# A state space stage with y kept transposed, D x added on TensorE, and its instructions emitted in the order of a list scheduler

## The chip, the cores and the metric

The kernel runs on one core of a Trainium2 chip. The metric is device time in microseconds (us) of one execution; the profile gives one profiled execution. Engines are named as in the profile: PE is TensorE (matmuls; PEld are its weight loads), DVE is VectorE, ACT is ScalarE, POOL is GpSimd, SP is SyncE, which here only issues DMAs. All data is fp32. In the trace every matmul of fp32 operands appears as two records, a transpose as one.

## The reference, cut to what matters

The input has 2 images of 256 channels and 48 x 48 positions. Layer 0 adds a local attention and depthwise convolutions. Layer 1 treats each image as 2304 tokens of 256 channels. It adds a state space model to the normalised tokens and then a mixture of 8 experts of which each token uses two. What the change touches is the state space model:

```python
xn = rmsnorm(x)                                   # x: (2, 2304, 256)
zxbcdt = einsum('bld,ed->ble', xn, W_in)
z, xBC, dt = zxbcdt[..., :512], zxbcdt[..., 512:1152], zxbcdt[..., -8:]
conv = sum(pad(xBC)[:, k:k + L, :] * conv_w[:, k] for k in range(4)) + conv_b
xBC = silu(conv)                                  # 512 of x, 64 of B, 64 of C
dt = softplus(dt + dt_bias)                       # 8 heads of 64 channels
dA = exp(dt * -exp(A_log))
state = state * dA_t + (dt_t * x_t) B_t           # scan over tokens
y_t = state C_t
y = (y + Dp * xs) * silu(z)
y = rmsnorm(y, gnorm_w, 1e-5)
out = x + einsum('ble,de->bld', y, W_out)
```

The experts follow on the normalised result: a gate picks the two experts of each token, and each expert is two matrix products with a gelu between them.

## The kernel before, in words

`run` has three stages that follow one another: `layer0`, `mamba` and `experts`. The change is in `mamba` and in a few lines around it.

`mamba` works on 12 blocks (`NBLK` 6 for each of two images) of 384 tokens, and each block on 3 chunks of 128 tokens, 36 chunks in all. Six front stages work on a block:

- `norms` (L590) transposes 3 x 2 pieces of the residual on PE, copies them out on ACT (L541), takes means and variances on DVE, and writes the new residual (L612) and the normalised tokens (L618) on DVE.
- `project_0` and `project_1` transpose the normalised tokens back, multiply by the weights of x, B and C (five products of 387 columns by `project`, L553), and do the four taps of the convolution: the last on ACT (L662), three on DVE (L666). Then come two silus on ACT (L649, L650). A DMA moves the rows of C to partitions 0 to 63 (L652).
- `gates_0` and `gates_1` compute z, dt and the gate's scores for each chunk, tokens on partitions: 2 x 2 products of 264 columns, a silu from PSUM (L679), and two small DVE operations (L683, L684); then `softplus` for dt.
- `sums` makes the cumulated decays with three small products and two exponentials.

Six stages work on a chunk:

- `token_stage` makes `al` on POOL (L744), transposes B and x on PE (L748, L751), copies them out on ACT (L753, L755), makes `xd` on DVE (L757) and `xw` and y = D x on POOL (L759, L761).
- `decay_stage` multiplies `al` by a triangle (two products of 512 columns, L769), takes the exponential on ACT (L778, `mt`), and multiplies by the masked B C product on DVE (L779).
- `state_stage` makes this chunk's addition to the state (L787) and the old state's part of y (L790), decays and adds the state on DVE (L795, L796) and scales the part of y on DVE (L798); POOL adds it to y (L799).
- `y_stage` is eight heads of 64 columns with `mt` as the weights (L808), an addition on DVE (L809), the product with z on POOL (L810), squares with a sum on ACT (L813), and an inverse root by `rsqrt` (L171 on DVE, L172 on POOL).
- `turn_stage` transposes y in four pieces (L539) and copies it on ACT (L541).
- `out_stage` multiplies by `W_out` and the gate's folded weights (L835, 264 columns), adds to the residual on DVE (L839), adds the gate's scores (L840), takes statistics (L844, L845), and stores the chunk by DMA (L846).

`gate` works on a group of 6 chunks (the last two groups have 3). It takes the two best experts of each token with some thirty small DVE operations, writes the normalised tokens (L871), counts with two small products (L905, L906), numbers the rows (L915, L916), and sends each chunk by two indirect DMAs that POOL issues (L926), 72 in all. `experts` begins with `plan` on those counts and reads the rows back.

What sets the order: in `mamba` a loop of steps calls the stages with written lags (front stages up to five steps ahead, `out_stage` four behind) and draws from the generator `gate` between them. The framework places every instruction on its engine's queue from this order and may move it; the engines then work through their queues in order and wait for semaphores. PSUM has 4 single banks and 2 pairs, shared by all three stages.

Of the kernel before, what the change touches and what calls it, by code (L numbers as in the profile page):

```python
# [30 lines left out]
F32 = mybir.dt.float32  # L31
# [5 lines left out]
P = 128  # L37
# [20 lines left out]
ZH = DI // 2  # L58

ZG = ZH + SH  # L60
XBC = 2 * ZG
# [4 lines left out]
GRP = 6  # L66
# [15 lines left out]
for _name, _k in (  # L82
    ("bq", NH), ("bk", NH), ("bv", NH), ("bp", 1), ("w1", NH * 9), ("w2", NH * 9), ("norm_w", NH),
    ("gnorm_w", DI // P), ("conv_w", NM * 4), ("conv_b", NM),
):
    _VEC[_name] = (_n, _n + _k)
    _n += _k
# [4 lines left out]
for _name, _k in (  # L92
    ("dt_bias", SH), ("A_log", SH), ("Dp", SH), ("bg", E), ("rate1", 1), ("rate2", 1),
):
    _ROW[_name] = (_n, _n + _k)
    _n += _k
# [17 lines left out]
def together(*streams):  # L114

    streams = list(streams)
    while streams:
        for s in list(streams):
            if next(s, StopIteration) is StopIteration:
                streams.remove(s)  # L120
        yield


def interleave(*streams):
    for _ in together(*streams):
        pass


class Kernel:
# [12 lines left out]


    def setup(self):
        nc, ins = self.nc, self.ins
        self.ps = self.pool("ps", 4, space=bass.MemoryType.PSUM)
        self.ps2 = self.pool("ps2", 2, space=bass.MemoryType.PSUM)
# [27 lines left out]
    def layer0(self, ctx):  # L175


        nc, ins, v, r = self.nc, self.ins, self.v, self.r
        wts = self.pool("l0w", 1, ctx)
# [314 lines left out]
    def mamba_weights(self):  # L494
# [4 lines left out]
        wout = wts.tile([P, DI // P, C + E], F32, name="wout")  # L499
# [5 lines left out]
        self.l1 = dict(win=win, wout=wout, na=na, sw=sw)  # L505

    def scale_weights(self):
# [3 lines left out]
        wg = [l1["win"][:, k, ZG + ZH : XBC] for k in range(NH)]  # L511
# [4 lines left out]
        for k in range(NH):  # L516
            for w in (l1["win"][:, k, : ZG + ZH], l1["win"][:, k, XBC:]):
                nc.gpsimd.tensor_scalar(w, w, v["norm_w"][:, k : k + 1], None, ALU.mult)
        turned = self.att.tile([P, NH, P], F32, tag="turned", name="turned", bufs=1)
        for m in range(DI // P):  # L520
# [34 lines left out]
    def mamba(self, ctx):  # L555


        self.m = self.pool("m", 2, ctx)
        self.blocks, self.chunks = {}, {}
        nblk, nchunk = B * NBLK, B * NBLK * NJ  # L560
        front = (self.norms, self.project_0, self.project_1, self.gates_0, self.gates_1, self.sums)
        stages = ((self.out_stage, 4), (self.turn_stage, 3), (self.y_stage, 2), (self.state_stage, 1),
                  (self.decay_stage, 1), (self.token_stage, 0))
        groups = [GRP] * (nchunk // GRP - 1) + [GRP // 2] * 2
        starts = [sum(groups[:n]) for n in range(len(groups))]
        gate = iter(())
        for step in range(-NJ * 2, nchunk + 4):
            for p in reversed(range(len(front))):
                k, r = divmod(step + len(front) - 1 - p, NJ)
                if r == 0 and 0 <= k < nblk:  # L570
                    front[p](k)
                    next(gate, None)
            for stage, lag in stages:
                c = step - lag
                if 0 <= c < nchunk:
                    if stage == self.out_stage and c in starts:
                        self.group = dict(first=c, n=groups[starts.index(c)])
                    stage(c)
                next(gate, None)
            done = step - 3  # L580
            if done in starts[1:] or done == nchunk:
                for _ in gate:
                    pass
                gate = self.gate(self.group)
        for _ in gate:
            pass


    def norms(self, k):

        nc, small = self.nc, self.small
        b, blk = divmod(k, NBLK)
        t = self.m.tile([P, NJ, C], F32, tag="t", name="t", bufs=2)
        st = small.tile([P, NJ, 6], F32, tag="lst", name="lst")
        mv = small.tile([P, NJ, 2], F32, tag="lmv", name="lmv")
        for j in range(NJ):
            cols = slice(blk * TB + j * P, blk * TB + (j + 1) * P)
            self.transposes(t[:, j, :], [self.x[b][:, h, cols] for h in range(NH)])
            nc.vector.bn_stats(st[:, j, :], t[:, j, :])
            nc.vector.bn_aggr(mv[:, j, :], st[:, j, :])  # L600
        mean, var = mv[:, :, 0], mv[:, :, 1]
        rs, ms, rr, rs1, mrs, kap = (
            small.tile([P, NJ], F32, tag=f"n{name}", name=name) for name in ("rs", "ms", "rr", "rs1", "mrs", "kap")
        )
        self.rsqrt(rs, var, 1e-5)
        nc.vector.tensor_mul(ms, rs, rs)
        nc.vector.tensor_mul(ms, ms, var)
        self.rsqrt(rr, ms, F32_EPS)
        nc.vector.tensor_scalar(rs1, rs, 1.0, None, ALU.add)
        nc.vector.tensor_mul(mrs, mean, rs)  # L610
        for j in range(NJ):
            nc.vector.tensor_scalar(  # L612
                self.residual(k * NJ + j), self.halves(t[:, j, :]), rs1[:, j : j + 1], mrs[:, j : j + 1],
                ALU.mult, ALU.subtract,
            )
        nc.vector.tensor_mul(rr, rr, rs)
        for j in range(NJ):
            nc.vector.tensor_scalar(  # L618
                t[:, j, :], t[:, j, :], mean[:, j : j + 1], rr[:, j : j + 1], ALU.subtract, ALU.mult
            )  # L620

        nc.vector.reciprocal(kap, rr)
        nc.vector.tensor_mul(kap, kap, rs1)
        msw = small.tile([P, NJ, E], F32, tag="msw", name="msw")
        nc.vector.tensor_tensor(msw, bcast(mean, 2, [P, NJ, E]), bcast(self.l1["sw"], 1, [P, NJ, E]), ALU.mult)
        self.blocks[k] = dict(t=t, kap=kap, msw=msw)

    def project_0(self, k):
        nc, block = self.nc, self.blocks[k]
        t = block.pop("t")  # L630
        xn = block["xn"] = self.m.tile([P, NH, TB + 3], F32, tag="xn", name="xn")

        if k % NBLK == 0:
            nc.vector.memset(xn[:, :, 0:3], 0.0)
        else:
            nc.vector.tensor_copy(xn[:, :, 0:3], self.blocks[k - 1]["xn"][:, :, TB:])
        for h in range(NH):
            self.transposes(xn[:, h, 3:], [t[:, j, h * P : (h + 1) * P] for j in range(NJ)])
        block["xc"] = self.m.tile([P, NM - 1, TB], F32, tag="xc", name="xc")
        block["bc"] = self.m.tile([P, TB], F32, tag="bc", name="bc", bufs=3)  # L640
        for m in range(2):
            self.convolve(block, m)

    def project_1(self, k):
        nc, block = self.nc, self.blocks[k]
        for m in range(2, NM):
            self.convolve(block, m)
        xc, bc = block["xc"], block["bc"]
        nc.scalar.activation(xc, xc, AF.Silu)  # L649
        nc.scalar.activation(bc, bc, AF.Silu)  # L650
        ct = block["ct"] = self.m.tile([DS, TB], F32, tag="ct", name="ct", bufs=3)
        nc.sync.dma_start(ct, bc[DS:P, :])  # L652

    def convolve(self, block, m):

        nc = self.nc
        xn, win = block["xn"], self.l1["win"]
        ps = self.bank()
        self.project(ps[:, : TB + 3], lambda k: win[:, k, XBC + m * P : XBC + (m + 1) * P], lambda k: xn[:, k, :])
        wc = self.v["conv_w"][:, 4 * m : 4 * m + 4]  # L660
        out = block["xc"][:, m, :] if m < NM - 1 else block["bc"]
        nc.scalar.activation(  # L662
            out, ps[:, 3 : TB + 3], AF.Identity, bias=self.v["conv_b"][:, m : m + 1], scale=wc[:, 3:4]
        )
        for i in range(3):
            nc.vector.scalar_tensor_tensor(out, ps[:, i : i + TB], wc[:, i : i + 1], out, ALU.mult, ALU.add)  # L666

    def gates(self, block, j):

        nc = self.nc  # L670
        xn, win = block["xn"], self.l1["win"]
        cols = slice(3 + j * P, 3 + (j + 1) * P)
        ps = self.banks()
        for h in range(2):
            self.project(
                ps[:, h, :ZG], lambda k: xn[:, k, cols], lambda k: win[:, k, h * ZG : (h + 1) * ZG]
            )
        z = block["z", j] = self.m.tile([P, DI], F32, tag="z", name="z", bufs=7)
        nc.scalar.activation(z.rearrange("p (h q) -> p h q", h=2), ps[:, :, :ZH], AF.Silu)  # L679
        if j == 0:  # L680
            block["dt"] = self.small.tile([P, NJ, SH], F32, tag="dt", name="dt")
            block["gp"] = self.small.tile([P, NJ, E], F32, tag="gp", name="gp")
# [577 lines left out]
```

## Time and profile before

| what | value |
|---|---|
| three timed runs: median (lowest to highest) | 1681.74 us (1681.54 to 1685.04) |
| profiled execution: time, span of its instructions | 1685.3 us, 1683.5 us |
| mean granted PE clock | 0.924 |
| busy over the span: PE, PEld, DVE, ACT, POOL | 1443.4, 1090.4, 926.1, 706.6, 580.6 us |
| first copy of `norms` to the first product of the experts (L541 to L1082) | 385.7 to 1073.1 us, so 687.4 us |
| busy from 385 to 1080 us: PE, PEld, DVE, ACT, POOL | 563.6, 371.4, 504.6, 308.4, 394.6 us |
| granted PE clock from 385 to 1080 us | 0.88 |

The span lies inside the time of the execution; 1.8 us lie around it. Busy time of PE counts records that overlap once; it depends on the granted clock, at which a product of the same shape takes up to twice as long. The experts take the span from 1073 us on and PE is busy there nearly without a gap.

### The profile page before, as it was taken

The page shows a single profiled execution, that of the slowest core. Times are in us where ns is not written, and L with a number is a line of the kernel's source. Part 1 is how long each engine was busy: PE and PEld are TensorE (multiplying, and loading weights), DVE is VectorE, ACT ScalarE, POOL GpSimd, SP SyncE. Part 2 cuts the span into 40 slices and gives each one's busy share as a digit, 9 for nine tenths or more (in the row PEclk, how much of TensorE's full clock was granted, in tenths as well). Part 3 has the DMA queues.
Part 4 walks back from the last instruction along what each step waited for, and adds up shares of the span by engine and source line. Part 5 has one row for each costly group of instructions (what it writes and reads, how often), then busy time and mean ns, then how long its engine had stood idle before and what let it go on. Part 6 is the DMA issues. An engine that isn't in the chain of part 4 may idle for free.

```text
span 1683.5 us, 20769 instructions
## 1 busy us (share of the span) xinstructions
PE 1443.4 (86%) x7188; PEld 1090.4 (65%) x7188; DVE 926.1 (55%) x2359; ACT 706.6 (42%) x1554; POOL 580.6 (34%) x596
## 2 busy tenths in 40 slices
PE   3788897877899889698897984499999999999994
PEld 1556565655556556465654653488888888888884
DVE  6688798985787868679687774211111111112113
ACT  0658584875655446355353520123223222322320
POOL 4111100201466565655656666221222122122220
PEclk9889998997999899798898976799999999999997
DMA  5312122211000010100101002577667666666747
GB/s 198 112 56 68 51 86 70 75 47 56 3 10 12 9 51 10 40 18 9 48 12 38 20 10 71 187 219 240 205 195 233 213 199 213 227 204 201 222 109 231
DMA packets 75689, 180.04 MB, mean 107 GB/s; under 512 B 8172, under 2 KB 66429, under 8 KB 69117
## 3 DMA queue, kind: packets, MB, share of 16 engines
q1 hardware_dynamic: 55660, 152.95, 26.3%
q0 software_dynamic: 14976, 20.26, 6.4%
q10 hardware_dynamic: 4948, 5.51, 1.0%
q8 instruction: 57, 0.93, 0.2%
q14 instruction: 48, 0.39, 0.1%
HBM read 140.40 MB, written 44.41 MB: 110 GB/s over the span
## 4 chain that ended last, share of the span: by engine, by line
PE 58%; DVE 18%; POOL 10%; ACT 7%; DMA 3%; issue 3%; SPq 0%; DVEq 0%; ACTq 0%; POOLq 0%
PE bank L1082 16%; PE po L1096 16%; PE bank L553 4%; DVE x L309 4%; POOL xs L926 3%; PE banks L553 3%; PE bank L808 2%; PE bank L835 2%; PE bank L539 2%; DVE hid L309 2%; PE bank L483 2%; ACT prob L440 2%; PE banks L769 1%; DVE prob L428 1%; PE bank L790 1%
## 5 line engine op out<-in xcount | busy, mean ns | idle before, releaser
L1086 ACT ACTIVATE hid<-bank,wt 128x256 f32<-128x256 f32 (+1 forms) x352 | 159.9, 455 | 405.2 <-PE bank L1082 401.3
L1082 PE MATMUL bank<-ext,wt 128*128 128x256 f32 (+1 forms) x1408 | 286.7, 362 | 2.6 <-DMA wt<-in_We 1.8
L1102 POOL DMA_INDIRECT acc<-ey,ex x80 | 124.9, 1562 | 463.6 <-DVE ey L1100 346.3
L1096 PE MATMUL po<-wt,hid 128*128 128x256 f32 x1280 | 283.7, 379 | 0.0
L1082 PEld LDWEIGHTS bank<-ext,wt 128*128 128x128 f32 x1408 | 250.1, 191 | 34.0 <-DVE ey L1100 2.1
L1096 PEld LDWEIGHTS po<-wt,hid 128*128 128x128 f32 x1280 | 239.8, 190 | 30.8
L541 DVE COPY ext<-bank 128x512 f32<-128x512 f32 (+1 forms) x44 | 28.3, 643 | 233.5 <-PE bank L539 233.5
L440 ACT ACTIVATE prob<-prob,top 128x308 f32<-128x308 f32 x144 | 78.4, 550 | 83.9 <-DVE top L428 83.8
L1099 DVE TENSOR_TENSOR ey<-po,wt 128x256 f32<-128x256 f32 x80 | 34.0, 424 | 143.8 <-PE po L1096 143.7
L309 DVE SCALAR_TENSOR_TENSOR x<-hid,w2r,x 128x1128 f32<-128x1128 f32 (+3 forms) x72 | 99.6, 1383 | 4.1 <-ACT hid L312 2.6
L553 PE MATMUL bank<-xn,win 128*128 128x387 f32 x240 | 95.4, 542 | 3.2 <-ACT xn L541 2.9
L360 POOL COPY kp<-kp 128x10 f32<-128x10 f32 (+1 forms) x60 | 22.5, 375 | 218.4 <-DVE kp L355 218.4
L483 PE MATMUL bank<-pt,val 110*64 110x128 f32 (+1 forms) x864 | 75.5, 297 | 23.0 <-DVE x L488 19.0
L666 DVE SCALAR_TENSOR_TENSOR xc<-bank,vec,xc 128x384 f32<-128x384 f32 x144 | 81.7, 611 | 21.4 <-ACT xc L662 20.9
L553 PE MATMUL banks<-win,xn 128*128 128x264 f32 x288 | 90.4, 449 | 0.0
L483 PEld LDWEIGHTS bank<-pt,val 110*64 110x64 f32 (+1 forms) x864 | 64.4, 147 | 39.2 <-DVE x L488 20.5
L926 POOL DMA_INDIRECT xs<-u,rows x72 | 75.6, 1051 | 35.2 <-issue 19.1
L309 DVE SCALAR_TENSOR_TENSOR hid<-xp,vec,hid 128x1128 f32<-128x1128 f32 (+3 forms) x64 | 87.3, 1374 | 0.3
L810 POOL TENSOR_TENSOR y<-y,z 128x512 f32<-128x512 f32 x36 | 47.0, 1306 | 107.2 <-DVE y L809 34.0
L744 POOL TENSOR_TENSOR al<-cst,a 128x1024 f32<-128x1024 f32 x36 | 68.6, 1913 | 42.1 <-DVE taken L916 14.1
L769 PE MATMUL banks<-al,cst 128*128 128x512 f32 x144 | 78.0, 641 | 5.3 <-ACT mt L778 4.7
L553 PEld LDWEIGHTS bank<-xn,win 128*128 128x128 f32 x240 | 50.6, 215 | 40.7 <-issue 9.5
(247 smaller groups left out, 2606.2 us busy)
## 6 DMA issues: line engine op xcount, KB each, us to landing
wt<-in_We SPq DMA_DIRECT2D x44, 2184.0 KB
ex<-xs SPq DMA_DIRECT2D x36, 265.0 KB
val<-vtab SPq DMA_DIRECT2D x72, 110.0 KB
x<-in_x SPq DMA_DIRECT2D x4, 1152.0 KB
vraster<-vout SPq DMA_DIRECT2D x18, 256.0 KB
acc<-x SPq DMA_DIRECT2D x36, 128.0 KB
vtab<-vraster SPq DMA_DIRECT2D x12, 304.0 KB
val<-vtab SPq DMA_DIRECT2D x36, 88.0 KB
```

The lines of the kernel that those rows point to most:

```text
L309: nc.vector.scalar_tensor_tensor(dst, src, w[:, k : k + 1], dst, ALU.mult, ALU.add)
L440: nc.scalar.activation(prob[:, a, :], prob[:, a, :], AF.Exp, bias=top[:, a : a + 1], scale=-1.0, accum_out=den[:, a : a + 1],)
L483: nc.tensor.matmul(po[j * HD : (j + 1) * HD, :P], lhsT=val[:nk, i, a * HD : (a + 1) * HD], rhs=pt[:nk, j, i, :], start=i == 0, stop=i == l ...
L553: self.nc.tensor.matmul(ps, lhsT=lhs(k), rhs=rhs(k), start=k == 0, stop=k == NH - 1)
L666: nc.vector.scalar_tensor_tensor(out, ps[:, i : i + TB], wc[:, i : i + 1], out, ALU.mult, ALU.add)
L744: nc.gpsimd.tensor_tensor(al, bcast(self.c["le"], 1, [P, SH, P]), bcast(block["a"][:, j, :], 2, [P, SH, P]), ALU.mult)
L769: nc.tensor.matmul(pd[:, k, :], lhsT=self.c["gt"], rhs=al[:, 4 * k : 4 * k + 4, :].rearrange("p s t -> p (s t)"), start=True, stop=True,)
L926: put = nc.gpsimd.indirect_dma_start(self.xs, bass.IndirectOffsetOnAxis(ap=rows[:, i, k : k + 1], axis=0), u2[:, i, :], None)
L1082: nc.tensor.matmul(ps[:, :rows], lhsT=w1[:, k, c * P : (c + 1) * P], rhs=xt[:, k, :], start=k == 0, stop=k == NH - 1,)
L1086: nc.scalar.activation(hid[:, c, :], ps[:, :rows], AF.Gelu, bias=b1[:, c : c + 1])
L1096: nc.tensor.matmul(po, lhsT=hid[:, c, j * P : (j + 1) * P], rhs=w2[:, c, :], start=c == 0, stop=c == NHC - 1)
L1102: put = nc.gpsimd.indirect_dma_start(self.acc, bass.IndirectOffsetOnAxis(ap=token, axis=0), y, None, compute_op=ALU.add)
```

## The change

In words, by the names of the new code:

- **y has its channels on partitions.** `y` is four pieces of 128 channels by 128 tokens. `py` takes `xd` as the weights (64 columns) and `mt` as the moving side (128 columns), two heads of a pair into the two halves of the output's partitions. D x is added in the same PSUM bank by a product with a diagonal matrix (`diag`, made once). z is computed with channels on partitions (four products of 384 columns for a block). `turn_stage`, the POOL operations L761 and L799 and the copy `xt` are gone.
- **The sum of squares** is taken by PE (`ss`: four products of one column with the squares as weights).
- **The state** lies on 128 partitions by 256 columns; its decay is on POOL (`decayed`). The old state's part of y is four products (`ps`). Its decay in time now varies along the free axis; it is made by a small product (`er`), an exponential (`from`), a store of 8 x 384 values to DRAM (`spread`), and two broadcasting loads for a chunk (`rd`, 256 KB).
- **Moves to ACT**: the residual (`sr`), the normalised tokens (`st`) and the gate's normalised tokens (`u2`), which were DVE's L612, L618 and L871.
- **dt and scores** of a block are one group of three 16-column products (`dg`).
- **ACT's tables**: the six silus of a block are a chain that nothing interrupts, and the table with exp and ln is loaded after it.
- **PSUM** pools are made for each stage; in `mamba` 4 single banks, 1 pair and 2 banks for z. **Groups** of the gate are 6, 6, 6, 6, 6, 4, 2.
- **Order**: every operation is added to `Flow` with an engine, a cost in ns, what it needs, and which buffers it takes and frees. `run` plays the engines forward in time and emits each operation when its engine is free, the most urgent first. For PE, DVE and ACT the framework keeps this order (`manual_schedule`); POOL and the DMA queues are not in that list.

The core of the diff:

```diff
-GRP = 6
+GROUPS = (6, 6, 6, 6, 6, 4, 2)
+class Flow:
+    HOP = 120
+    def rank(self):
...
+            tail[k] = o["cost"] + max(same, default=0) + self.HOP
+        return {k: o["due"] - tail[k] for k, o in self.ops.items()}, after
+    def run(self):
...
+            for k in sorted(ready, key=lambda k: rank[k]):
+                o = ops[k]
+                if ready[k] > now or busy.get(o["engine"], 0) > now:
+                    continue
+                kinds = [kind for kind, _ in o["takes"]]
+                if any(free[kind] < kinds.count(kind) for kind in kinds):
+                    continue
...
+                o["make"]()
 def mamba(self, ctx):
+        room = dict(bank=4, banks=1, zbank=2, cvbank=1, t=2, xn=2, xc=2, bc=3, ct=3, z=2, al=2, btt=2, xd=3, xw=2,
+                    mt=2, gm=2, y=4, sq=2, state=3, rd=3, u2=2)
...
+        with self.tc.manual_schedule(
+            engines={mybir.EngineType.PE, mybir.EngineType.DVE, mybir.EngineType.Activation}
+        ):
+            self.flow.run()
+    PACE = 11000
...
+        op("al", "POOL", 1940, al, ("s5", k), takes=[("al", c)])
+        op("pd", "PE", 880, pd, ("al", c), takes=[("banks", ("pd", c))], uses=[("al", c)])
+            def from_state():
+                ps, old = [self.bank_for(("ps", c, g)) for g in range(2)], T["state", c - 1]
+                for m in range(2):
+                    for g in range(2):
+                        rows = slice(g * DS, (g + 1) * DS)
+                        nc.tensor.matmul(
+                            ps[g][:, m * P : (m + 1) * P], lhsT=old[rows, m * P : (m + 1) * P],
+                            rhs=(T["bc", k][rows, cols] if g else T["ct", k][:, cols]), start=True, stop=True,
+                        )
...
+            op("rd", "queue", 2800, rd, ("spread", k), takes=[("rd", c)])
+            op("ps", "PE", 450, from_state, ("state", c - 1), ("ct", k), ("rd", c), takes=[("bank", ("ps", c, 0)), ("bank", ("ps", c, 1))],
+               uses=[("state", c - 1)] + ([("bc", k)] if last else []))
+            op("decayed", "POOL", 750, decayed, ("state", c - 1), ("ex", k), takes=[("state", c)],
+               uses=[("state", c - 1)])
+        def py():
+            ps = self.bank_for(("py", c))
+            for m in range(NZ):
+                part = slice(m * P, (m + 1) * P)
+                for i in range(2):
+                    s = 2 * m + i
+                    nc.tensor.matmul(
+                        ps[i * HD : (i + 1) * HD, part], lhsT=T["xd", c][:, s * HD : (s + 1) * HD],
+                        rhs=T["mt", c][:, s, :], start=True, stop=False,
+                    )
+                nc.tensor.matmul(
+                    ps[:, part], lhsT=self.l1["diag"][:, m, :], rhs=T["xc", k][:, m, cols], start=False, stop=True
+                )
...
+        op("py", "PE", 1800, py, ("mm", c), ("xd", c), None if fresh else ("yi", c), takes=[("bank", ("py", c))],
+           uses=[("mt", c), ("xd", c)] + ([("xc", k)] if last else []))
...
+        op("ss", "PE", 880, ss, ("sq", c), takes=[("bank", ("ss", c))], uses=[("sq", c)])
+        op("out", "PE", 920, out, ("yz", c), ("rs", c), takes=[("bank", ("out", c))], uses=[("y", c)])
+                op(("put", (c, q)), "POOL", 1100, put, ("g10", g), ("g8", g), ("u2", c), ("number", c), uses=[("u2", g)])
```

A chunk's operations are due at 11 us times its number (`PACE`), and a group's gate at the time of its last chunk plus three.

## The prediction

> **What bounds the kernel now.** I first read the busy time over the span, then the busy time in stretches of the state space stage, cut where a group of 6 chunks ends.
>
> ```profile
> PE 1443.4 (86%) x7188; PEld 1090.4 (65%) x7188; DVE 926.1 (55%) x2359; ACT 706.6 (42%) x1554; POOL 580.6 (34%) x596
> ```
>
> ```profile
> core 0: us, PE busy (x) PEld busy (x) DVE busy (x) ACT busy (x) POOL busy (x), PEclk, DMA share, GB/s
> 385.00:561.00 176.00, 155.35 (x650) 100.37 (x649) 133.87 (x355) 99.55 (x169) 83.13 (x69) 0.92 0.06 21
> 561.00:669.00 108.00, 91.51 (x389) 60.48 (x388) 83.97 (x227) 51.50 (x88) 66.20 (x60) 0.92 0.08 25
> 669.00:775.50 106.50, 90.48 (x385) 59.40 (x384) 79.87 (x225) 50.90 (x88) 64.95 (x60) 0.90 0.08 25
> 775.50:883.40 107.90, 92.54 (x388) 60.16 (x387) 82.83 (x227) 51.09 (x88) 66.26 (x59) 0.91 0.08 25
> 883.40:993.00 109.60, 93.64 (x392) 60.30 (x390) 83.80 (x210) 45.76 (x77) 77.00 (x70) 0.91 0.08 25
> 993.00:1073.00 80.00, 33.17 (x126) 24.88 (x125) 37.87 (x171) 6.37 (x15) 37.01 (x39) 0.62 0.18 60
> ```
>
> The columns are the stretch, its length, and busy time by engine, then PE's granted clock. In the four middle stretches PE is the busiest, 85%, but at clock 0.91. Busy time times clock is PE's work at full clock: 84.2, 81.4, 84.2 and 85.2 us, mean 83.8, so 13.96 us for a chunk, while a chunk takes 432 / 24 = 18.0 us. For 36 chunks the work is 503 us, and the stage lasts 687.4 us (385.7 to 1073.1). So 185 us are PE standing or PE slow: about 33 in the first stretch (176 less 155.35 x 0.92), 97 in the middle ones (432 less 335), 55 in the tail. That is all that a better order can win.
>
> Where it stands shows in the timeline. POOL first, then PE, at the end of a group:
>
> ```profile
> 698.63 1.09 POOL L926 DMA_INDIRECT xs<-u,rows  x1 [0.92 <-DVE rows L923]
> 700.02 0.96 POOL L926 DMA_INDIRECT xs<-u,rows  x1 [0.30 <-issue]
> ...
> 709.86 1.27 POOL L810 TENSOR_TENSOR y<-y,z 128x512 f32<-128x512 f32 x1
> ```
>
> ```profile
> 704.60 0.27 PE L748 MATMUL bank<-cst,bc 64*128 64x64 f32 x1
> 712.33 1.11 PE L751 MATMUL bank<-cst,xc 128*128 128x128 f32 x4 [7.46 <-DVE gm L776]
> ```
>
> The gate's 12 indirect DMAs stand in one row on POOL, 1.27 us each. The chunks' own POOL work waits behind them, and PE stands 7.5 us. What follows is slow as well. The same eight heads, before and after a pause of 9 us:
>
> ```profile
> 1009.99 1.90 PE L808 MATMUL bank<-xd,mt 128*128 128x64 f32 x16
> ...
> 1026.17 3.51 PE L808 MATMUL bank<-xd,mt 128*128 128x64 f32 x16
> ```
>
> **The change, PE's work.** I take the distance of starts of consecutive matmul records at full clock. 128x128 transposes: 0.109 us. 264 columns: 0.222. 387 columns: 0.325. 64 columns behind 128-column weights (L808): 0.112, so this is the least that a full weight load costs. Two products in different halves of the weight columns (L483, 128 columns) come 0.057 apart, half of 0.109, so they run side by side. So do two in different halves of the rows: the score products (L422) start 0.006 apart in pairs. A step from whole columns to half columns costs: L464 to L464 is 0.109, L464 to L483 0.202, so 0.093 for a switch. For a chunk:
>
> - transposes of y go: 4 x 0.109 = -0.44;
> - z, dt and scores, for a block: 24 x 0.222 = 5.33 become 16 x 0.322 (L329, 384 columns) + 12 x 0.112 = 6.50; by three, +0.39;
> - `er`: 6 x 0.109 for a block, +0.22;
> - state (L787: 0.48 + 0.52) becomes two pairs of 256 columns (0.215 by L1082) = 0.43, -0.57; the old state's part (L790: 0.53 + 0.43) becomes four pairs of 0.109, -0.52;
> - `py`: 16 x 0.112 = 1.79 become 16 x 0.057 + 8 x 0.109 + 8 switches x 0.093 = 2.52, +0.73;
> - `ss`: eight weight loads of 0.112, +0.90.
>
> Together +0.71 us, by 36 = +26 us: PE's work is 528 us, 14.67 for a chunk. No record shows a burst of four half-column products between switches; between full overlap without switch cost (-27 us) and no overlap (16 x 0.052 x 36 = +30 us) I take the rows as they stand.
>
> **The other engines**, for the stage. DVE (504.6 us) loses L612 13.1, L618 23.4, L871 21.4 and L795 32.7, and about 9 of L796's 23.0, whose rows halve: about 405, or 11.3 for a chunk. The two half-width `yi` are bounded by L798's 685 ns and two of L839's 469; I count no change. ACT (308.4) loses `xt` 21.2, `yt` 21.1, the read of the sum 6.8, and table loads: 70 of 1.283 us become two for a block, 24, so 89.9 to 30.8. It gains 108 normalisations, between the copy of 256 columns (0.384) and the biased 384 columns (0.673); I take 0.45, nearer to the first: +49. Sum about 255, with `from` +6. POOL (394.6) loses 45.0 + 40.4 and gains 34 decays, between half of L759's 1.075 and all of it, say 0.75: +26, so 335, 9.3 for a chunk. All three lie under PE's 14.7, and none lies on the path if the order is good. `rd` is bounded by landings in the chain of waits, 2.5 us (the last store) to 8.2 us (384 KB of `x<-acc`); three buffers let it start a chunk or more ahead, so I count nothing. If late, `yi` waits on DVE, and the convolution taps queued behind it hold the PSUM banks that PE needs next. The four `diag` operations run on POOL at the start, which waits there for 9.3 us before 29.2; ahead of that gap they cost at the worst 1 us.
>
> **The order.** Its gain is what it leaves of the 185 us. Every put is now an operation of its own, due three chunks late, so other POOL work may come between; the stop of 7.5 us and the slow time behind it should mostly go. I take 5 us of loss for a group, as the remaining small waits in the third stretch add up to (L787 2.1, L751 0.4, L769 1.1, L539 1.6): 20 for the middle. First stretch 20 instead of 33, since the first norms and the first slow products stay. Tail 40 instead of 55: the last group has 2 chunks instead of 3 (two puts, 2.5 us), and no puts of 15 us stand before the last chunks; the path through `plan` and the fetch stays. Sum: 528 + 20 + 20 + 40 = 608, against 687.4: -79. The profiled execution, 1683.5 + 1.8, would be 1606; the median of the runs is 3.6 lower: **1602**.
>
> **A rule of the Trainium skill against my floor.** In the stage PEld is busy 371 of 695 us, 53%. "Perfetto Trace Analysis", Identifying the Most-Contended Engine, says that matmul busy time is a bad measure and weight load time a better one. By it PE would have half its time free and DVE's 405 us would be the floor: the stage would be 405 + 80, the time about 1479. The stretches speak against it: in the experts PE stands for nothing and PEld is at 85%, because a 256-column product outlasts its weight load.
>
> A second rule, "TensorEngine Tiling (Array Packing)", Key Properties, says that changing the tiling mode drains the engine, which speaks against `py`. It gives no price; without one the sum would be 27 us lower.
>
> **Rivals.**
>
> - *The pauses stay* (slower). POOL isn't among the engines whose order is kept; if its 12 puts still stand in a row, `xw`, `al`, and now the state's decay wait behind 15 us of them. Then the 185 us stay and the 26 us of PE work come on top: 1682 + 26 = 1708. For it: POOL's row above, and the decay which DVE did before. Against: puts are spread in the emitted order. It decides when less than 26 of the 185 us go.
> - *The planned costs are wrong.* `pd` is planned at 880 ns and `out` at 920, but four records of 512 columns take 4 x 0.43 = 1.72 and eight of 264 take 1.78. PE is 1.7 us late on every chunk. If PE itself is the bound this is harmless. If the queues that are written for the shorter costs each time make it wait once as long, 36 x 1.7 = 61: 1663.
> - *PE packs better*: half-column products overlap without switch cost (-27) and losses of 15 + 5 + 35 stay: 1602 - 27 - 25 = 1550.
> - *The change doesn't do all it says*: if the table loads stay at 70, ACT has 314 us instead of 255, 8.7 for a chunk, still under 14.7. The time stays in the forecast's own case.
>
> **Chances.** The forecast's own case (1560 to 1645) 0.62, better packing 0.08, wrong costs 0.17, slower 0.11, no change 0.02. The first three are faster: 0.87. A measurement of this kernel can tell about 0.2% from no change. Eight in ten: 1553 to 1657, which leaves out half of better packing, the slower case and a little of the third.
>
> **What would show it.** Right: the distance between groups falls from 108 to about 93 us; PE's clock in the middle is over 0.97; PE's busy time in the stage is about 535 us; 24 table loads; no two puts in a row longer than three. Wrong: a gap of several us on PE beside a row of L926's successors on POOL, a clock near 0.9, `py` far from 2.5 us, or DVE busier than PE.

## The result, and the profile after

The changed kernel takes **1699.91 us** (median of 4 runs, 1698.21 to 1701.85) beside 1683.12 us for the kernel before on the same chip (1681.54 to 1685.04): a ratio of 1.010, 95% interval 1.0081 to 1.0118. It is 1% slower; the forecast was 1602 us. The profiled execution spans 1696.4 us, against 1683.5.

The busy times of the whole span, which answer to the first line of the prediction:

```profile
PE 1495.4 (88%) x8016; PEld 1110.0 (65%) x8016; DVE 873.4 (51%) x2234; ACT 670.2 (40%) x1524; POOL 497.7 (29%) x564
```

DVE, ACT and POOL all do less, as foreseen. PE is busy 52 us longer. The stage, cut where a group's gate starts (columns as in the prediction's stretches: length, busy time by engine, PE's clock, DMA):

```profile
385.00:1086.00 701.00, 611.35 (x3145) 385.07 (x3143) 449.68 (x1283) 269.23 (x491) 307.82 (x313) 0.91 0.13 41
385.00:520.00 135.00, 123.33 (x627) 77.33 (x625) 85.34 (x254) 67.96 (x126) 46.65 (x45) 0.95 0.12 40
520.00:633.00 113.00, 102.24 (x528) 63.50 (x526) 75.77 (x206) 44.37 (x83) 51.80 (x53) 0.92 0.13 38
633.00:745.60 112.60, 101.88 (x526) 63.53 (x526) 74.90 (x206) 43.76 (x82) 51.18 (x52) 0.92 0.12 36
745.60:862.00 116.40, 106.61 (x518) 67.44 (x518) 73.03 (x204) 43.59 (x81) 51.36 (x53) 0.87 0.12 37
862.00:963.00 101.00, 92.46 (x510) 58.79 (x510) 69.97 (x180) 36.88 (x66) 49.83 (x51) 0.98 0.14 44
```

Two things show. A group still takes 101 to 116 us, where 93 was forecast (108 before). And PE is 90% busy in a middle stretch, so this is not a kernel that waits more than before: it works more. Taken at each instant from PE's records and the granted clock, the stage (from 385 us to the end of PE's wait for the experts' first rows) splits like this; "lost to the clock" is busy time times what is missing to full speed:

| us | stage ends | PE idle | lost to the clock | PE's work at full clock |
|---|---|---|---|---|
| before | 1071.2 | 130.6 | 55.6 | 500.0 |
| after | 1084.2 | 88.9 | 49.6 | 560.7 |
| forecast | | 80 together | | 528 |

The change won 48 us of idle and slow time and paid 61 us of new PE work. The sum is the 13 us by which the span grew; the rest of the span is 612.3 us in both. So two questions are left: where 61 us of work come from instead of 26, and why 139 us are still lost instead of 80.

**The lost time.** One group's end, on POOL (start, duration, then the instruction):

```profile
677.45 1.08 POOL L1327 DMA_INDIRECT xs<-u,rows  x1 [4.07 <-DVE ss L1164]
678.57 0.57 POOL L1189 TENSOR_TENSOR rg<-ss,half 128x1 f32<-128x1 f32 x1
679.33 1.04 POOL L1327 DMA_INDIRECT xs<-u,rows  x1 [0.18 <-issue]
...
692.06 0.96 POOL L1327 DMA_INDIRECT xs<-u,rows  x1 [0.30 <-issue]
693.04 0.62 POOL L1084 TENSOR_TENSOR state<-state,ex 128x256 f32<-128x256 f32 x1
693.61 3.75 POOL L986 TENSOR_TENSOR al<-cst,a 128x1024 f32<-128x1024 f32 x2
```

on DVE,

```profile
694.09 4.36 DVE L1049 TENSOR_TENSOR mt<-mt,gm 128x1024 f32<-128x1024 f32 x1
...
698.90 0.74 DVE L1100 TENSOR_TENSOR y<-bank,rd 128x256 f32<-128x256 f32 x2
```

and on PE:

```profile
699.36 0.66 PE L999 MATMUL bank<-cst,xc 128*128 128x128 f32 x4 [3.28 <-DVE y L1100]
```

The twelve puts still stand in a row, 1.27 us apart, with one small operation between. Two `al` come out behind the row together. DVE's masking L1049, which takes 1.2 us at its fastest and 1.5 at the median, takes 4.36 us beside them, and PE, which needs a bank that DVE holds behind it, stands 3.3 us. "SBUF — State Buffer", SBUF: two separate sides, of the Trainium skill says that a VectorE operation with two SBUF inputs and a GpSimd operation that reads SBUF lock each other out for whole instructions; the overlap of L986 (693.61 to 697.36) with L1049 agrees. After the wait PE is at half clock for 10 us, and so at the same place of the group before:

```profile
588.10:598.30 10.20, 10.20 (x35) 5.02 (x36) 5.48 (x7) 1.02 (x1) 3.61 (x5) 0.50 0.09 26
700.70:710.90 10.20, 10.20 (x35) 4.99 (x36) 5.53 (x7) 1.02 (x1) 3.62 (x5) 0.50 0.09 27
813.40:833.90 20.50, 19.55 (x84) 12.94 (x85) 10.09 (x21) 1.87 (x3) 9.03 (x8) 0.50 0.00 1
```

PE is busy all that time, and still slow.

**The work.** Products of y at full clock; the numbers at the head are start and modelled duration:

```profile
759.31 0.44 PE L1124 MATMUL bank<-mt,xd 128*64 128x128 f32 x4
759.67 0.49 PE L1128 MATMUL bank<-xc,diag 128*128 128x128 f32 x2
760.09 0.44 PE L1124 MATMUL bank<-mt,xd 128*64 128x128 f32 x4
```

From start to start, one pair of heads with its D x takes 0.36 + 0.42 = 0.78 us, so y takes 3.1 us for a chunk where 2.52 were forecast.

### The profile page after: what moved, and what is told of

Its sections match the earlier page's. It is cut to its first block, busy times and chain, and to the rows that moved or that the text cites. A ratio compares the mean times of both kernels' runs of the same rounds, so it can differ in the third digit from the quotient of the medians.

```text
span 1696.4 us, 22488 instructions
## 1 busy us (share of the span) xinstructions
PE 1495.4 (88%) x8016; PEld 1110.0 (65%) x8016; DVE 873.4 (51%) x2234; ACT 670.2 (40%) x1524; POOL 497.7 (29%) x564
## 5 line engine op out<-in xcount | busy, mean ns | idle before, releaser
L1486 PEld LDWEIGHTS bank<-ext,wt 128*128 128x128 f32 x1408 | 250.0, 191 | 31.8 <-DVE ext L615 1.2
L837 DVE SCALAR_TENSOR_TENSOR xc<-bank,vec,xc 128x384 f32<-128x384 f32 x144 | 88.6, 615 | 34.2 <-ACT xc L826 31.2
L1032 ACT ACTIVATE mt<-banks 128x1024 f32<-128x1024 f32 x36 | 36.8, 1023 | 147.1 <-PE bank L1124 134.5
L627 PE MATMUL zbank<-xn,win 128*128 128x384 f32 x192 | 76.8, 535 | 12.5 <-ACT z L933 12.5
L1327 POOL DMA_INDIRECT xs<-u,rows x72 | 71.2, 989 | 39.0 <-issue 15.8
L1143 POOL TENSOR_TENSOR y<-y,z 128x512 f32<-128x512 f32 x36 | 47.5, 1320 | 117.2 <-DVE y L1137 71.5
L986 POOL TENSOR_TENSOR al<-cst,a 128x1024 f32<-128x1024 f32 x36 | 69.0, 1929 | 32.7 <-PE banks L1026 17.6
L1128 PE MATMUL bank<-xc,diag 128*128 128x128 f32 x288 | 78.0, 357 | 0.0
```

Source lines behind the costliest of these rows:

```text
L627: self.nc.tensor.matmul(ps, lhsT=lhs(k), rhs=rhs(k), start=k == 0, stop=k == NH - 1)
L837: nc.vector.scalar_tensor_tensor(out(), T["bank", ("cv", at)][:, i : i + TB], wc[:, i : i + 1], out(), ALU.mult, ALU.add)
L986: nc.gpsimd.tensor_tensor(self.large_tile("al", c, [P, SH, P]), bcast(self.c["le"], 1, [P, SH, P]), bcast(T["a", k][:, j, :], 2, [P, SH, P ...
L1128: nc.tensor.matmul(ps[:, part], lhsT=self.l1["diag"][:, m, :], rhs=T["xc", k][:, m, cols], start=False, stop=True)
L1327: ins = nc.gpsimd.indirect_dma_start(self.xs, bass.IndirectOffsetOnAxis(ap=of("rows")[:, i, q : q + 1], axis=0), T["u2", g][:, i, :], None,)
L1486: nc.tensor.matmul(ps[:, :rows], lhsT=w1[:, k, c * P : (c + 1) * P], rhs=xt[:, k, :], start=k == 0, stop=k == NH - 1,)
```

## The experiments

Three theories. **Theory 1**: PE's work was mis-sized, above all the switches between half and whole columns in y. **Theory 2**: the row of puts on POOL makes the pauses and the slow clock. **Theory 3**: the plan is wrong, since its costs are. The lines quoted carry each kernel's own line numbers.

**1. D x in half columns.**

```diff
-                nc.tensor.matmul(
-                    ps[:, part], lhsT=self.l1["diag"][:, m, :], rhs=T["xc", k][:, m, cols], start=False, stop=True
-                )
+                for i in range(2):
+                    half = slice(i * HD, (i + 1) * HD)
+                    nc.tensor.matmul(
+                        ps[half, part], lhsT=self.l1["diag"][:, m, half], rhs=T["xc", k][:, m, cols],
+                        start=False, stop=True,
+                    )
```

> The D x product is done as two products of half the columns each, as the head products are; everything else, the emitted order too, is that of the changed kernel. Theory 1 (the time went into PE work, 0.58 us a chunk of it into switches between half and whole columns): one chunk's products of y fall from 3.10 us to 1.8 to 2.0 us at full clock, PE's work in the stage from 561 to 515 to 520 us, and since PE is the bound nearly all of it comes back: 1655 to 1665 us. Theory 2 (PE waits at every group for POOL, whose 12 puts stand in a row): PE's work falls as much, but PE then stands longer at the same places, and the time stays above 1685 us. Theory 3 (the order is wrong because the planned costs are wrong): the plan is the same, so the waits stay where they are; 1665 to 1690 us.

Measured: 1649.38 us (ratio to before 0.9799, 0.9779 to 0.9819), 50 us under the changed kernel. y at full clock:

```profile
702.58 0.39 PE L1130 MATMUL bank<-xc,diag 128*64 128x128 f32 x4
702.80 0.39 PE L1124 MATMUL bank<-mt,xd 128*64 128x128 f32 x4
703.02 0.39 PE L1130 MATMUL bank<-xc,diag 128*64 128x128 f32 x4
```

That is below the forecast of every theory. There are more instructions, and each pair of heads with its D x takes 0.44 us instead of 0.78: 1.90 us for a chunk. Its four half-column records of D x add 0.22 us, as much as two whole ones 0.109 us apart would, so nearly all of the 0.34 us that are saved were the price of switching. PE's work in the stage is 522.8 us (-38). The rest of the 50 us is the clock's: idle time rose by 8 us, and what the slow clock costs fell from 49.6 to 30.2. Theory 1 stands; theory 2's claim, that the freed time would come back as waits, fails.

**2. Puts spread over the next chunks**, with POOL held to the order of the list, and **3. the control**, with POOL's order held and nothing else (of the edit, the line that spreads the puts):

```diff
-                op(("put", (c, q)), "POOL", 1100, put, ("g10", g), ("g8", g), ("u2", c), ("number", c), uses=[("u2", g)])
+                op(("put", (c, q)), "POOL", 1100, put, ("g10", g), ("g8", g), ("u2", c), ("number", c),
+                   ("xw", min(NCHUNK - 1, first + n + 3 + i)), uses=[("u2", g)])
```

> Two puts of a group may be issued only after the weighting of x of one further chunk, and POOL keeps the order of the list, so that in the middle groups no more than two puts stand together (the last two groups keep rows of 8, 8 and 4). PE's work is unchanged. Theory 1 (PE work is what was mis-sized): the loss of the stage falls by no more than 10 us of its 140; 1688 to 1700 us. Theory 2 (the row of puts is the pause): in five groups the idle time of 3 to 9 us beside the row and about 5 us of slow clock behind it go; 1650 to 1670 us. Theory 3: within 5 us of the changed kernel, 1695 to 1705 us.

> Control for the run with spread puts: POOL keeps the order of the list, and nothing else is changed, so the 12 puts of a group still stand in a row with one operation between. If the row of puts is the pause: within 6 us of the changed kernel, 1693 to 1705 us, and the gain of 35 us belongs to the spreading. If POOL's order was disturbed in other ways, and the gain came from keeping it: 1660 to 1675 us.

Measured: spread 1664.88 us (0.9899, 0.9874 to 0.9925); control 1695.82 us (1.0085, 1.007 to 1.0101). Spreading is worth 31 us, holding the order 4 us. In the control the puts of a middle group still stand in rows of 11 or 12, so the row is in the emitted list itself. POOL in the run with spread puts:

```profile
651.76 1.09 POOL L1340 DMA_INDIRECT xs<-u,rows  x1 [0.18 <-issue]
653.15 0.97 POOL L1340 DMA_INDIRECT xs<-u,rows  x1 [0.30 <-issue]
...
654.70 0.61 POOL L1097 TENSOR_TENSOR state<-state,ex 128x256 f32<-128x256 f32 x1
655.27 3.74 POOL L999 TENSOR_TENSOR al<-cst,a 128x1024 f32<-128x1024 f32 x2
```

and its first and last middle stretch; over the four, PE's clock is 0.95 to 1.00, where it was 0.87 to 0.98:

```profile
520.90:623.90 103.00, 96.34 (x517) 61.07 (x516) 67.85 (x196) 41.52 (x76) 45.40 (x47) 0.95 0.12 34
...
830.10:925.80 95.70, 90.23 (x510) 58.08 (x509) 67.05 (x179) 37.09 (x66) 51.53 (x51) 1.00 0.15 46
```

The loss of these four groups is 33 us, against 73 in the changed kernel (idle time 24 against 40, slow clock 9 against 33), with the same work (372 and 370 us). The longest masking on DVE takes 2.32 us, where it was 4.63. Theory 2 stands for the middle of the stage, and theory 1 alone, which gave this run no more than 10 us, does not explain it.

**4. The plan's costs as the trace has them.**

```diff
-        op("pd", "PE", 880, pd, ("al", c), takes=[("banks", ("pd", c))], uses=[("al", c)])
+        op("pd", "PE", 1820, pd, ("al", c), takes=[("banks", ("pd", c))], uses=[("al", c)])
...
-        op("out", "PE", 920, out, ("yz", c), ("rs", c), takes=[("bank", ("out", c))], uses=[("y", c)])
+        op("out", "PE", 1870, out, ("yz", c), ("rs", c), takes=[("bank", ("out", c))], uses=[("y", c)])
...
```

> Only numbers of the plan are changed: the costs of the products of the mask (880 to 1820 ns), of the output (920 to 1870), of y (1800 to 3100), of the state (450 to 580 and 650), of the decays' rows (650 to 750) and of the normalisations (400 to 590) are those of the changed kernel's trace. Theory 3 (the order is wrong because the planned costs are wrong): PE's idle time in the stage falls from 90 to 40 to 60 us, and the time to 1640 to 1675 us. Theory 1: PE is the bound in either order; 1690 to 1702 us. Theory 2: the puts come out in shorter rows as well (12, 5, 2, 5 in place of 12 each), so some of its gain comes too: 1675 to 1690 us.

Measured: 1717.65 us (1.0208, 1.0191 to 1.0226), 18 us **slower** than the changed kernel; no theory expected that. The waits of PE begin with

```profile
PE bank L1159 <- ACT sq L1184: 23.3, 6, 7.1
```

(total, times, longest). In the third group, on POOL and then on PE:

```profile
671.29 0.96 POOL L1327 DMA_INDIRECT xs<-u,rows  x1 [0.30 <-issue]
672.27 1.27 POOL L1143 TENSOR_TENSOR y<-y,z 128x512 f32<-128x512 f32 x1
```

```profile
674.26 1.87 PE L1159 MATMUL bank<-ones,sq 128*128 128x1 f32 x8 [5.35 <-ACT sq L1184]
```

The gate product L1143 (y times the silu of z) comes out behind ten puts; ACT squares it, and PE, whose order is fixed, stands at the sum of squares. The plan with true costs had put a more urgent operation where the row of puts is. PE's work is unchanged (560.2 us); idle time rose by 13 us and the clock's cost by 7.

**5. The order not held** on PE, DVE and ACT (the context around `self.flow.run()` taken away).

> The operations are emitted in the same order, but TensorE, VectorE and ScalarE are no longer held to it. Theory 1: the kept order earned the 48 us by which the loss of the stage fell, so without it the time is 1720 us or more. Theory 2: the pauses are POOL's, whose order isn't held in either; 1690 to 1710 us. Theory 3 (a wrong plan is worse than none): 1650 to 1685 us.

Measured: 1736.0 us (1.0315, 1.0257 to 1.0374): 36 us above the changed kernel. Idle time is 99.1 us, and the clock costs 87.4. That loss, 186.5 us, is the one of the kernel before (186.2), beside the changed kernel's work (556.1): so the 48 us were won by the kept order, as theory 1 had it. It is worth having, even with its wrong costs.

**6 to 8. Both, then with the measured costs, then with a wider pace** (`PACE = 14500`). The cost of `py` is 1900 with half columns.

> Both: D x in half columns and the puts spread over the next chunks, POOL's order kept. If the switches and the row of puts are two causes that add up (-50 and -35 us): 1610 to 1620 us, PE's work in the stage about 525 us, its loss 95 us. If the half columns gained in part what the spread gains too (the shorter products left less to wait for; PE's slow clock fell in both, by 19 and by 25 us): 1620 to 1640 us.

> The same with the plan's costs as the traces have them (mask 1820 ns, output 1870, y 1900, state 580 and 650, rows 750, normalisations 590). With true costs alone the stage became 19 us longer, since the sums of squares then stood just where the row of puts holds up the gate product of the same chunk (PE waits up to 7.5 us there). If that was the whole reason, then with spread puts true costs gain: 5 to 20 us under the run without them, 1595 to 1612 us. If a plan that packs PE fully is worse because it leaves nothing for durations that vary: 5 to 20 us over it.

> As before, with due times 14.5 us a chunk apart in place of 11: about PE's work for a chunk. If the due times push the front of the pipeline too far ahead of its consumers, which then wait for PSUM banks: 5 to 15 us under the run with true costs alone. If the rank is decided by the path behind an operation and not by the due times: within 4 us of it.

Measured: 1636.83 us (0.9733, 0.9719 to 0.9746); with the costs 1626.88 us (0.9669, 0.9655 to 0.9682); with the pace 1647.01 us (0.9793, 0.9778 to 0.9808). The two causes don't add up: 50 and 35 us alone, 63 together. The same split as above shows why: what the slow clock costs could be had only once. It is 49.6 us in the changed kernel, 30.2 with half columns, 24.1 with spread puts, and 29.0 with both. With spread puts and half columns, true costs gain 10 us instead of losing 18; that sign was foreseen, the 1595 to 1612 us weren't reached. The due times do count, more than either expectation had it: at 14.5 us a chunk, about PE's own pace, the time is 20 us longer. The cause stays open.

**9. D x left out; 10. three of four products of the sum of squares left out.** Both price a part by its absence.

> The changed kernel with D x left out of y (its product isn't computed at all), so that only the 8 head products are left; order and plan unchanged. It prices the whole of what moving D x to TensorE costs. By PE's work: one chunk's y falls from 3.10 us to 16 x 0.057 = 0.9 us, 79 us for 36 chunks, and with the slow clock that fell by 19 us in the run with half columns: 1600 to 1620 us. By the prediction's rows (8 x 0.109 and 8 switches of 0.093, 1.6 us a chunk): 58 us, 1635 to 1645 us. If POOL's row of puts sets the pace: not below 1640 us.

> The changed kernel with three of the four products of each sum of squares left out (the sum covers the first 128 channels alone). It takes 6 of the 8 weight loads of a chunk, 6 x 0.112 = 0.67 us, 24 us of PE's work in all, and no switch with them. PE is the bound: 1670 to 1680 us. PE's time is worth little, since it waits for others: 1688 to 1700 us.

Measured: 1632.04 us (0.9702, 0.9687 to 0.9717) without D x, PE's work 494.6 us (-66), and 1672.06 us (0.9937, 0.9922 to 0.9952) with one product of squares, PE's work 539.7 us (-21). The time without D x lies between what the two ways of counting gave, nearer to the prediction's rows (58 us of work and 1635 to 1645 us) than to the other (79 us, 1600 to 1620 us). D x in whole columns costs 68 us of time; in half columns it costs 1649.4 - 1632.0 = 17. The sum of squares was priced closely at 0.112 us for a weight load (24 us of work expected, 21 measured); its time came back somewhat more than whole (28 us for 21), the clock's share falling by 12 us and idle time rising by 7.

**11. Spread puts and true costs with D x in whole columns.**

> Spread puts and the plan's costs as measured (y 3100 ns), D x in whole columns as in the changed kernel: the half columns' worth once the puts and the plan are mended. By PE's work alone (38 us, as the trace of the run with half columns had it): 1660 to 1670 us, against 1627 with half columns. If the switches also hold the clock low wherever y follows a wait: 1670 to 1690 us.

Measured: 1668.67 us (0.9921, 0.9906 to 0.9936), 42 us above the same with half columns, and inside what PE's work alone gave. In the two profiled executions, 35 us apart, it is 38 us of work and 12 us of slow clock (43.6 against 31.8), less 14 us of idle time. Beside the run with spread puts alone (1664.88 us, whole columns too) the true costs gain nothing: the ratios, 0.9921 and 0.9899, overlap in their intervals. Idle time fell by 15 us there, and what the slow clock costs rose by 20.

**12. Shorter last groups on top** (`GROUPS = (6, 6, 6, 6, 5, 3, 2, 2)`, puts of the last ones four to a chunk).

> Half columns, spread puts, costs as measured, and the last groups cut as 5, 3, 2, 2 chunks in place of 6, 4, 2, with the puts of the last three groups spread four to a chunk: in the plan no row is longer than four. If the rows of 8 puts at the end still hold the last chunks' gate products (PE waits 9 us there for the squares, 10 us for the counts): 1612 to 1622 us. If the tail is set by the last group's own chain (gate, puts, plan, first fetch): within 4 us of 1627 us.

Measured: **1619.39 us** (0.962, 0.9607 to 0.9634), the fastest: 63 us under the kernel before and 80 under the changed one. It lies where it was expected if the rows of eight puts still held up the last chunks: PE's longest wait for the squares is 2.4 us, where it was 7.4 in run 7. Its wait for the experts' first rows fell too, from 21.5 to 17.1 us, so the two ways aren't cleanly separated.

What the slow clock and idle time still cost in its stage is 99 us: 19 in the first stretch, 38 in the middle, 42 in the tail.

## Why the prediction was wrong

- **What bounds the stage: right.** PE does. The work that each edit took from PE came back as time (38 us of work for 50 of time, 66 for 68, 21 for 28). The rule on weight loads would have called 450 us of DVE the floor.
- **`py`, "2.52": wrong, and most of the missing work.** The terms for the products held: the heads alone take 1.02 us in the run without D x, with one way in and out. The step that failed is "8 switches x 0.093". Starts of records in y lie, for a pair of heads and its D x, 0.007, 0.153, 0.007, 0.203, 0.213 and 0.205 us apart; in half columns throughout it is 0.103 and 0.007 in turn. So a switch costs 0.10 on the way in and 0.10 on the way out, and the second product behind each switch comes late too, by 0.05 (half columns) and 0.10 (whole). That is 0.35 us for two switches, not 0.186: 0.17 each. Over 36 chunks y's miss is (3.10 - 2.52) x 36 = 21 us. The trace before already showed the second delay: at each of the 19 steps from L483 back to L464 that run at full clock without a wait the first whole product comes 0.20 us after the last half one, and the next one 0.16 us later instead of 0.109. The prediction took the first of these and not the second.
- **State and old state, "-0.57" and "-0.52": wrong for the same reason.** `ps` takes 0.645 us instead of 0.44 and `pst` 0.583 instead of 0.43. Their products lie in half rows or half columns between whole ones, so each burst has a way in and a way out, and I charged neither: (0.205 + 0.153) x 36 = 13 us. In a burst of `ps` the second product comes 0.21 us after the first, the third 0.11 us after the second:

```profile
582.23 0.37 PE L1077 MATMUL bank<-ct,state 64*128 64x128 f32 x1
...
582.44 0.27 PE L1077 MATMUL bank<-ct,state 64*128 64x128 f32 x1
...
582.55 0.27 PE L1077 MATMUL bank<-ct,state 64*128 64x128 f32 x1
```

  With y that is 34 us, most of the 35 that PE's work missed. That the two agree so closely is partly luck: by the same starts of records z, dt and scores came to 6.81 us for a block instead of 6.50 and the outputs to 1.87 us for a chunk instead of 1.78, 7 us more, and the measure by busy time recovers somewhat less than these distances (38 us for half columns, where they give 43).
- **`ss`, "+0.90": right** (0.88); the z, dt and scores products were close (6.81 us for a block, 6.50 forecast).
- **The other engines:** the table loads fell from 70 to 28, two for a block as forecast and four more in the first block. DVE has 450 us instead of 405, ACT 269 instead of 255 (a normalisation takes 0.592 us, not the 0.45 that lay "nearer to the first"; the planned 0.40 is further off still), POOL 308 instead of 335. All lie under PE, so none of this moved the time by itself.
- **"The order": first stretch right** (17.8 us lost, 20 forecast), **tail near** (47.7, 40; in the kernel before it was 57, not 55), **middle wrong** (73, 20). The failed step is "Every put is now an operation of its own ... so other POOL work may come between". It may, but where nothing else is ready on POOL at that moment the list emits all twelve at once, the more so as they are all due at the same time; `al` and the gate product come ready while the row runs and wait behind it. So "puts are spread in the emitted order", which the prediction held against its slower rival, was not so: the control keeps that order on POOL, and its rows are of 11 and 12. Spread, the middle loses 33 us; the largest wait left in that run ahead of the experts' first rows is PE's for ACT's silus of z (`zbank`, 13.4 us in sum), which the prediction didn't name.
- **The rivals.** *The pauses stay* named the right mechanism and came within 8 us of the time, but not by its own sum: it left all 185 us in place and 26 us of work on top; in truth 48 us went and 61 came. Its point of decision ("less than 26 of the 185 us go") wasn't what decided. *The planned costs are wrong* is refuted as a cause of the slowness: true costs alone make it worse, and are worth 10 us only where the row is gone and D x is in half columns. *PE packs better* is what the version with half columns does, by another way than the forecast had in mind.
- **The scale.** With the two failed steps mended (half columns, spread puts) and the costs set, the same change gives 1627 us, and 1619 with shorter last groups: 55 to 63 us of the forecast's gain of 80 were there, and two pieces of the change spent them.

## What to carry to other kernels

When products of half and whole columns alternate on TensorE, count a price per switch in both directions (here 0.17 us), also for a short burst between others; a few more instructions in one tiling can be cheaper than fewer in two. A list scheduler keeps what it plans only if its fill-in work can wait: twelve small operations with one due time become one block of 15 us on the engine that others need, so give each its own earliest place. And mend a plan's pauses before its costs: here true costs alone put urgent work where the row of puts was and lost 18 us, and gained 10 only with both other repairs.

## What the runs showed of the hardware

- **Half clock can outlast the wait before it.** "TensorE: Matmul & The Clock Gate", What's actually happening, of the Trainium skill gives full clock after one busy window of about 3.4 us. With half columns most slow stretches are 3.4 us long. In the first two below, of that kernel, PE is busy throughout; the other two are the 10 us behind each, at full clock:

```profile
567.00:570.40 3.40, 3.40 (x7) 1.77 (x6) 0.56 (x3) 1.50 (x2) 2.78 (x5) 0.50 0.41 130
676.20:679.60 3.40, 3.40 (x7) 1.67 (x6) 2.44 (x2) 1.38 (x4) 2.89 (x4) 0.51 0.02 4
570.40:580.00 9.60, 8.75 (x68) 5.46 (x66) 6.04 (x11) 3.72 (x7) 7.03 (x6) 1.00 0.10 29
679.60:690.00 10.40, 9.47 (x94) 6.87 (x95) 9.62 (x18) 1.77 (x3) 6.35 (x5) 1.00 0.12 36
```

  In the changed kernel the stretches shown above last 10.2 and 20.5 us with PE 95 to 100% busy, so the page's rule does not hold there. Those long ones all hold y's alternating products; the two short ones hold mostly products of z, 384 columns wide. But y isn't needed for a long one. In the tail of the run with spread puts PE is busy for 13.7 us at half clock with sums of squares, output products and one burst of state products, and no product of y (1002.1 to 1015.8 us, clock 0.50). With both repairs one stretch of 10.2 us remains in the middle, and it holds y in half columns. Whether y's switches make such stretches longer, and what ends them, no run separates.
- **Two repairs of the slow clock share one loss.** Half columns took 19 us of it, spread puts 25, both together 21.
